# Inverse roots moved from GpSimd to ScalarE and VectorE in the first stage of a stack of graph layers

## The chip, the cores and the metric

The kernel runs on one core of a Trainium2 chip. The core has five engines with queues of their own: TensorE (PE) multiplies matrices, VectorE (DVE), ScalarE (ACT) and GpSimd (POOL) work on elements, and SyncE (SP) issues transfers. Each queue is worked off strictly in the order in which the program was written, and an instruction that needs another engine's result waits at the head of its queue. The metric is the device time of one execution in microseconds (us), the median of several runs.

## The reference

The input is `x`, 128 batches of 128 tokens with 128 features, and an adjacency matrix `adj` of 128 x 128 integers for each batch. Four graph layers follow each other. Each normalises `x` over its features (mean and variance), takes the positive part, puts it through the layer and adds the result to `x`. Cut to what matters here:

```python
def _layernorm(x, eps=1e-5):
    return (x - mean(x)) / sqrt(var(x) + eps)

h = maximum(_layernorm(x), 0)                 # layer 0
agg = sum over r of (mask_r / degree_r) @ h @ rel_weights[r]
out = agg + h @ self_w.T + self_b
x = x + relu((out - mean) * rsqrt(var + 1e-5) * ln_gamma + ln_beta)

h = maximum(_layernorm(x), 0)                 # layer 1
D = abs(h[:, :, None, :] - h[:, None, :, :])  # all pairs of tokens
s = leaky(batch_norm(D @ W1.T)) @ W2.T        # norm over all pairs of all batches
A = softmax(where(adj > 0, s, NEG))
y = leaky(batch_norm((A @ h) @ Wg.T))
x = x + concat(h, y) @ Wt.T
```

Layers 2 and 3 are attention layers with the mask `adj > 0`. So the first stage needs three norms for each token: of `x`, of the first layer's output, and of the `x` that results. It also needs the mask as bytes for the later layers.

## The kernel before, in words

The batches are worked in 32 groups of four (`G = 4`). Tokens lie on the 128 partitions; a tile of a group is 128 x 512.

The first stage does layer 0 for all groups and, at the same time, the pairwise products of layer 1. These two threads are the functions `chain` and `pairs`.

`pairs(i)` handles one of 512 tiles, four to a batch (`NT = 4`), sixteen to a group. `difference` (line 312) forms a 128 x 2048 tile `d` of differences, on VectorE for tiles 0 and 2 of a batch and on GpSimd for tiles 1 and 3 (`ON_POOL`). `absolute` (L360) takes absolute values on ScalarE, except for tile 0, which uses a maximum and extra products instead. `products` (L322, L325) multiplies on PE into PSUM. `evacuate` (L336) copies the result `hp` to `z` on ScalarE. `statistics` (L350 to L357) reads `z` on VectorE. Full halves of `z` are written to memory.

`chain(g)` handles layer 0 for a group. Its steps, with their engines, are: load `x` and `adj` (SP); `mask` (Pool, L449); moments of `x` (VectorE); inverse root and shift (Pool, `roots`); `hn` (ScalarE, `centred`, L462), which is the normalised positive part; transposition, projection and gathering (PE), with evacuations on ScalarE (L475); `joined` (VectorE, L489); moments of the output; inverse root and shift again; `oc` (ScalarE, L462); scale, offset, positive part and sum (VectorE, L493 to L497); moments of the new `x`; inverse root and shift a third time; and `h1` (ScalarE, L503), the input of layer 1. `m8` (Pool, L527) stores the mask as bytes. `features` turns `h1` into `xe` and `xw` (L394, L402), which the difference tiles and products use.

The inverse root is the helper `rsqrt` (L225, L226), which adds the epsilon and raises to the power -0.5 on GpSimd. `shift` (L281, L282) multiplies the mean by it and negates. Each works on 128 x 4 values, one for each token of a batch.

The order is written out by hand-made planning. Every piece of work is registered by `step(name, engine, cost, after, rank, work)` with a planned cost in us. `_ordered` plays the engines forward: it takes the step that can start first, with 0.4 us for each change of engine (`HOP1`), and settles ties on an engine by the rank. The resulting list is the program's order, so a changed cost or a changed step can move the work around it. Groups 0 and 1 have their chains in an opening part, which also looks for relation numbers above 1 and ends in a branch. The other 30 chains run between the pair tiles. The lines that a norm's steps come from are these:

```python
step(("rs", g), "Pool", 1.95, own("mv"), s0 + 5, roots)
step(("hn", g), "ACT", 1.55, own("rs"), s0 + 7, lambda: centred("hn", "x", AF.Relu))
```

After the first stage come a stage for layer 1's scores and sums, and one for layers 2 and 3. They use `rsqrt` too, and are not part of the change.

Of the kernel before, what the change touches and what calls it, by code (L numbers as in the profile page):

```python
# [9 lines left out]
F32 = mybir.dt.float32  # L10
# [3 lines left out]
AF = mybir.ActivationFunctionType  # L14
OP = mybir.AluOpType
AX = mybir.AxisListType

P = 128
G = 4
EPS = 1e-5  # L20
# [148 lines left out]
def tile_gnn_stack(ctx: ExitStack, tc: tile.TileContext, a: dict, out: bass.AP):  # L169
    nc = tc.nc  # L170
# [3 lines left out]
    const = ctx.enter_context(tc.tile_pool(name="const", bufs=1))  # L174
    res = ctx.enter_context(tc.tile_pool(name="res", bufs=1))
    small = ctx.enter_context(tc.tile_pool(name="small", bufs=4))
# [11 lines left out]

    ident = const.tile([P, P], F32, name="ident")
    make_identity(nc, ident)  # L190
    mhalf = const.tile([P, 1], F32, name="mhalf")
    nc.gpsimd.memset(mhalf, -0.5)
    ones = const.tile([P, P], F32, name="ones")
    nc.vector.memset(ones, 1.0)

# [21 lines left out]
    M8 = [res.tile([P, G, P], U8, tag=f"m{g}", name=f"m{g}") for g in range(NG)]  # L217
    MV1 = res.tile([P, NG, G, 2], F32, name="MV1")
    RS1 = res.tile([P, NG, G], F32, name="RS1")
# [3 lines left out]
    def rsqrt(dst, var):  # L223

        nc.gpsimd.tensor_scalar(dst, var, EPS, None, op0=OP.add)  # L225
        nc.gpsimd.tensor_tensor(dst, dst, mhalf[:, 0:1].to_broadcast(list(dst.shape)), OP.pow)  # L226
# [35 lines left out]
    with tc.tile_pool(name="c0", bufs=1) as c0, tc.tile_pool(name="p0", bufs=2) as p0, ExitStack() as ctx0:  # L262
# [11 lines left out]

        XP = [psum.tile([P, 4, P], F32, tag=f"xp{n}", name=f"xp{n}") for n in range(2)]
        gamma, beta = (t[:, 2, :] for t in XP)

        def shift(mv, rs):

            nb = small.tile([P, G], F32, name="lnnb")  # L280
            nc.gpsimd.tensor_tensor(nb, mv[:, :, 0], rs, OP.mult)  # L281
            nc.gpsimd.tensor_scalar(nb, nb, -1.0, None, op0=OP.mult)  # L282
            return nb

# [9 lines left out]
        def step(name, engine, cost, after, rank, work, takes=(), gives=()):  # L296
            steps.append((name, engine, cost, after, takes, gives, rank, work))
# [113 lines left out]
        def chain(g, agg=None, again=None):  # L411

            bs = slice(g * G, g * G + G)
            s0 = G * NT * g - 31
            t = {}
            own = lambda *names: [(name, g) for name in names]

            def tile0(name, dtype=F32, **kw):
                pool, tag = p0, name
                if again is not None:  # L420

                    pool, tag = again, {"mask": "mask4", "maskT": "adjT", "o": "adjf"}.get(name, name)
                    kw = dict(bufs=2) if name == "hn" else {}
                t[name] = pool.tile([P, G, P], dtype, tag=tag, name=name, **kw)
                return t[name]
# [8 lines left out]
            def moments(name):  # L434
                st = small.tile([P, G, 6], F32, name="lnst")
                mv = t["mv"] = MV1[:, g] if name == "MV1" else small.tile([P, G, 2], F32, name="lnmv")
                src = t["x" if name == "MV1" else name]
                for k in range(G):
                    nc.vector.bn_stats(st[:, k, :], src[:, k, :])
                for k in range(G):  # L440
                    nc.vector.bn_aggr(mv[:, k, :], st[:, k, :])

            def roots(last=False):
                rs = t["rs"] = RS1[:, g] if last else small.tile([P, G], F32, name="lnrs")
                rsqrt(rs, t["mv"][:, :, 1])
                t["nb"] = shift(t["mv"], rs)

            def masked():
                nc.gpsimd.tensor_scalar(tile0("mask"), t["adj"], 1, None, op0=OP.is_equal)  # L449
# [8 lines left out]
            def centred(dst, src, func=AF.Identity):  # L458
                if dst not in t:
                    tile0(dst)  # L460
                for k in range(G):
                    nc.scalar.activation(t[dst][:, k, :], t[src][:, k, :], func, bias=t["nb"][:, k:k + 1],  # L462
                                         scale=t["rs"][:, k:k + 1])

            def shared():
                nc.gpsimd.tensor_tensor(t["mask"], t["mask"], t["deg"][:, :, None].to_broadcast([P, G, P]),
                                        OP.mult)

            def turned(src):
                t["pt"] = sm("pt")  # L470
                for k in range(G):
                    nc.tensor.transpose(t["pt"][:, k, :], t[src][:, k, :], ident)

            def copied(name, src, func=AF.Copy):
                nc.scalar.activation(tile0(name), t[src], func)  # L475
# [34 lines left out]
            else:  # L510
# [1 line left out]
            step(("mask", g), "Pool", 1.5, own("load"), s0 + 1, masked)  # L512
            step(("mv", g), "DVE", 1.05, own("load"), s0 + 3, lambda: moments("x"))
            step(("deg", g), "DVE", 0.6, own("mask"), s0 + 3.1, degree)
            step(("rs", g), "Pool", 1.95, own("mv"), s0 + 5, roots)
            step(("most", g), "Pool", 0.25, own("deg"), s0 + 5.1, at_least)
            step(("per", g), "DVE", 0.15, own("most"), s0 + 7, lambda: nc.vector.reciprocal(t["deg"], t["deg"]))
            step(("hn", g), "ACT", 1.55, own("rs"), s0 + 7, lambda: centred("hn", "x", AF.Relu))
            step(("share", g), "Pool", 1.05, own("per"), s0 + 9, shared)
            step(("pt", g), "PE", 0.55, own("hn"), s0 + 9, lambda: turned("hn"), takes=("sm",))  # L520
            step(("hT", g), "ACT", 0.5, own("pt"), s0 + 9.5, lambda: copied("hT", "pt"), gives=("sm",))
            step(("pm", g), "PE", 0.55, own("share", "hT"), s0 + 11, lambda: turned("mask"), takes=("sm",))
            step(("maskT", g), "ACT", 0.5, own("pm"), s0 + 12, lambda: copied("maskT", "pt"), gives=("sm",))
            step(("ph", g), "PE", 1.05, own("hT") + ["small"], s0 + 11.1, projected, takes=("sm",))
            step(("hw", g), "ACT", 0.5, own("ph"), s0 + 13, lambda: copied("hw", "ph"), gives=("sm",))
            step(("m8", g), "Pool", 1.5, own("load"), s0 + 11,
                 lambda: nc.gpsimd.tensor_scalar(M8[g], t["adj"], 0, None, op0=OP.is_gt))  # L527
            step(("po", g), "PE", 2.05, own("maskT", "hw"), s0 + 14, gathered, takes=("sm",))
            step(("o", g), "DVE", 0.6, own("po", "agg") + ["selfb"], s0 + 15, joined, gives=("sm",))
            step(("mvo", g), "DVE", 1.05, own("o"), s0 + 15.1, lambda: moments("o"))  # L530
            step(("rso", g), "Pool", 1.95, own("mvo", "hn"), s0 + 17, roots)
            step(("oc", g), "ACT", 1.55, own("rso"), s0 + 18, lambda: centred("o", "o"))
            step(("on", g), "DVE", 1.25, own("oc") + ["on_all"], s0 + 20, scaled, takes=("sm",))
            step(("end", g), "DVE", 0.62, own("on"), s0 + 21, ended, gives=("sm",))
            step(("x", g), "SP", 0.4, own("end") + [("part", PARTS - 1)], s0 + 21.1, lambda: nc.sync.dma_start(X[g], t["x"]))
            step(("mvx", g), "DVE", 1.05, own("end"), s0 + 21.1, lambda: moments("MV1"))
            step(("rsx", g), "Pool", 1.95, own("mvx", "oc", "m8"), s0 + 23, lambda: roots(True))
            for half in range(2):
                step(("h1", g, half), "ACT", 0.78, own("rsx") + [("xp", 2 * g - 5)] + [("h1", g, 0)] * half,
                     s0 + 25 + half, lambda half=half: h1(half))  # L540


# [103 lines left out]
        with tc.If(nc.values_load(flag, min_val=0, max_val=1) > 0) as cmp, \  # L646
# [6 lines left out]
            for g in range(NG):  # L653
                x = pr.tile([P, G, P], F32, name="x")
                nc.sync.dma_start(x, a["x"][g * G:g * G + G].rearrange("b t c -> t b c"))
                adj = pr.tile([P, G, P], I32, name="adj")
# [3 lines left out]
                hT = pr.tile([P, G, P], F32, name="hT")  # L660
# [3 lines left out]
                o = pr.tile([P, G, P], F32, name="o")  # L664
# [107 lines left out]
    with tc.tile_pool(name="bn", bufs=1) as bn:  # L772
# [3 lines left out]
        last = bn.tile([P, 1], F32, name="last")  # L776
# [41 lines left out]
    with tc.tile_pool(name="c1", bufs=1, reuse_waits="tile") as c1, \  # L818
# [8 lines left out]
        own = c1.tile([P, 1], F32, name="own")  # L827
# [19 lines left out]
        for n in range(2):  # L847
            t = c1.tile([P, G, 1 + 2 * KH], F32, name=f"sk{n}")
# [776 lines left out]
```

## Time and profile before

| what | us |
|---|---|
| median of 3 runs | 2777.38 |
| lowest and highest run | 2776.46, 2777.83 |
| profiled execution, its own time | 2781.11 |
| its span, first to last instruction | 2779.3 |
| first stage's tiles, about | 42 to 1528 |
| of these 1486 us: VectorE busy | 1405.6 |
| ScalarE busy | 1379.5 |
| GpSimd busy | 1365.4 |
| PE busy | 1357.8 |

A profile lists every instruction with its engine, start and duration. An engine's busy time in a stretch is the time in which at least one of its instructions was running. Neighbouring instructions of an engine overlap a little, so the distance between two starts is often less than the duration. What ended an idle time is called its releaser. The chain is found by going back from the last instruction to what released it, step by step; "issue" in it is time for which the profile shows no wait. Lines such as L312 are lines of the kernel's file.

### The profile page before, as it was taken

To read this page: it belongs to the slowest core of one execution; us is meant where nothing else is said; L and a number is where in the kernel's file an instruction comes from. 1 tells how busy PE (TensorE), PEld (TensorE's weight loads), DVE (VectorE), ACT (ScalarE), POOL (GpSimd) and SP (SyncE) were. 2 spreads that over 40 slices of the span, in tenths; PEclk is the share of its full clock that TensorE was granted. 3 is DMA by queue.
4 is the path that set the end of the run, shared out by engine and by line. 5 is a ranking of instruction groups with operands and counts; after the bars stand their busy time and mean duration, and the time that the engine had idled before them with its cause. 6 is when DMAs were issued, how large, how long until landed. Compare 5 with 4: busy or idle time off the path is not lost.

```text
span 2779.3 us, 42065 instructions
## 1 busy us (share of the span) xinstructions
PE 2457.4 (88%) x14521; PEld 1182.0 (43%) x14521; DVE 2472.0 (89%) x4712; ACT 2388.7 (86%) x2837; POOL 1724.0 (62%) x1629
## 2 busy tenths in 40 slices
PE   3899999999999999999998789888888897999896
PEld 2333333333333333333332344444444445777675
DVE  4899999999999999999999688888888887899976
ACT  4899999999999999999998778778778766899985
POOL 5799999999999999999997001111000115565642
PEclk7999999999999999999999899999999999999998
DMA  7455555555555555555543899999999971121110
GB/s 283 171 223 201 212 201 210 210 212 201 208 201 208 211 209 207 208 207 215 206 193 125 330 409 411 410 411 410 409 410 410 409 266 54 46 69 58 58 31 25
DMA packets 195933, 635.66 MB, mean 229 GB/s; under 512 B 32755, under 2 KB 100470, under 8 KB 132214
## 3 DMA queue, kind: packets, MB, share of 16 engines
q1 hardware_dynamic: 195264, 632.62, 58.6%
q8 instruction: 120, 1.97, 0.3%
q14 instruction: 111, 0.91, 0.1%
q10 hardware_dynamic: 438, 0.17, 0.0%
HBM read 328.84 MB, written 303.89 MB: 228 GB/s over the span
## 4 chain that ended last, share of the span: by engine, by line
ACT 33%; PE 22%; DVE 19%; issue 11%; DMA 10%; POOL 3%; SPq 1%; ACTq 0%; DVEq 0%; POOLq 0%
ACT d L360 11%; ACT z L336 11%; PE hp L322 6%; PE ps L871 5%; DMA rows<-sk 4%; DVE d L312 3%; DMA u<-rows 3%; DVE z L914 3%; DMA z<-hp 3%; PE hp L325 2%; ACT h L1229 2%; PE pk L878 2%; PE pv L1345 2%; ACT o L462 1%; ACT h L503 1%
## 5 line engine op out<-in xcount | busy, mean ns | idle before, releaser
L312 POOL TENSOR_TENSOR d<-xe 128x2048 f32<-128x2048 f32 x256 | 1074.1, 4202 | 67.1 <-PE hp L322 48.9
L322 PE MATMUL hp<-d,w1T 128*64 128x512 f32 x4096 | 999.4, 603 | 119.8 <-ACT z L336 96.8
L360 ACT ACTIVATE d<-d 128x2048 f32<-128x2048 f32 x384 | 734.6, 1935 | 24.7 <-POOL d L312 18.2
L312 DVE TENSOR_TENSOR d<-xe,xp 128x2048 f32<-128x2048 f32 x256 | 579.5, 2264 | 5.8 <-PE hp L322 3.1
L322 PEld LDWEIGHTS hp<-d,w1T 128*64 128x64 f32 x4096 | 286.2, 137 | 640.4 <-issue 466.6
L336 ACT COPY z<-hp 128x1024 f32<-128x1024 f32 x512 | 516.9, 1028 | 47.1 <-PE hp L325 24.4
L962 POOL TENSOR_TENSOR x<-x,bt 128x512 f32<-128x512 f32 x32 | 46.5, 1455 | 672.1 <-DMA x<-x 629.0
L350 DVE BATCH_NORM_STATS2 st<-z 128x6 f32<-128x512 f32 x512 | 349.3, 682 | 42.4 <-ACT z L336 42.1
L351 DVE BATCH_NORM_STATS2 st<-z 128x6 f32<-128x512 f32 (+1 forms) x512 | 329.3, 643 | 0.0
L914 DVE SCALAR_TENSOR_TENSOR z<-z 128x2048 f32<-128x2048 f32 x128 | 296.6, 2317 | 6.5 <-ACT z L896 6.5
L896 ACT ACTIVATE z<-z,bias,scale 128x2048 f32<-128x2048 f32 x128 | 267.1, 2087 | 9.3 <-DVE bias L809 7.7
L325 PE MATMUL hp<-both_t,xw 128*64 128x512 f32 x1024 | 268.3, 596 | 0.0
L900 ACT ACTIVATE zr<-z,bias,scale 128x2048 f32<-128x2048 f32 x128 | 267.3, 2088 | 0.9 <-DMA z<-hp 0.9
L871 PE MATMUL ps<-z,w2z 128*32 128x512 f32 x1024 | 144.7, 638 | 65.1 <-DVE z L914 64.9
L878 PEld LDWEIGHTS pk<-pick,su 128*128 128x128 f32 x1024 | 127.4, 196 | 136.2 <-DVE su L892 94.0
L878 PE MATMUL pk<-pick,su 128*128 128x16 f32 x1024 | 139.9, 269 | 19.9 <-DVE su L892 19.3
L1345 PE MATMUL pv<-wr,e 128*128 128x128 f32 x1024 | 141.7, 285 | 5.8 <-DVE e L1322 4.0
L871 PE MATMUL ps<-z,w2l 128*32 128x512 f32 x1024 | 142.7, 626 | 0.0
L871 PE MATMUL ps<-zr,w2r 128*32 128x512 f32 x1024 | 141.0, 623 | 0.0
L325 PEld LDWEIGHTS hp<-both_t,xw 128*64 128x64 f32 x1024 | 80.7, 138 | 140.7 <-issue 140.7
L1345 PEld LDWEIGHTS pv<-wr,e 128*128 128x128 f32 x1024 | 129.4, 197 | 13.5 <-DVE e L1322 4.1
L1322 DVE SCALAR_TENSOR_TENSOR e<-e,ps 128x512 f32<-128x512 f32 x160 | 106.8, 677 | 25.9 <-ACT ps L1319 25.1
(243 smaller groups left out, 3823.2 us busy)
## 6 DMA issues: line engine op xcount, KB each, us to landing
hp<-z SPq DMA_DIRECT2D x248, 1024.0 KB, 3.9
z<-hp SPq DMA_DIRECT2D x248, 1024.0 KB, 14.2
x<-x SPq DMA_DIRECT2D x118, 256.0 KB, 5.9
u<-rows SPq DMA_DIRECT2D x32, 384.0 KB, 11.6
x<-in_x_dram SPq DMA_DIRECT2D x32, 256.0 KB, 3.1
adj<-in_adj_dram SPq DMA_DIRECT2D x32, 256.0 KB, 3.5
part<-in_adj_dram SPq DMA_DIRECT2D x16, 512.0 KB, 7.6
out_dram<-x SPq DMA_DIRECT2D x32, 256.0 KB, 2.4
```

What stands on the lines that cost most here:

```text
L312: eng.tensor_tensor(d, ahead, x[:, None, None, :].to_broadcast([P, 2, KC, P]), OP.max if t == BY_MAX else OP.subtract)
L322: nc.tensor.matmul(hp[64 * hh:64 * hh + 64, c:c + 512], w1T2 if by_max else w1T, d[:, hh, c:c + 512], start=True, stop=not by_max, skip_gr ...
L325: nc.tensor.matmul(hp[64 * hh:64 * hh + 64, c:c + 512], XW[i // NT // 2][:, i // NT % 2, :], both_t.rearrange("p h k i -> p h (k i)")[:, h ...
L336: nc.scalar.copy(half_of(b, t), linear.pop(i))
L350: nc.vector.bn_stats(st[:, 2 * t, :], hs[:, 0:512])
L351: nc.vector.bn_stats(st[:, 2 * t + 1, :], hs[:, 512:1024 - P * last])
L360: nc.scalar.activation(diffs[i], diffs[i], AF.Abs)
L871: nc.tensor.matmul(ps[32 * c:32 * c + 32, :], w[:, w0:w0 + 32], v[:, 512 * c:512 * c + 512], start=j0 == 0, stop=w is w2r, skip_group_chec ...
L878: nc.tensor.matmul(pk[:, kk, 0:16], su[:, kk, :], pick.rearrange("p h j -> p (h j)"), start=True, stop=True)
L900: nc.scalar.activation(zr, z1, AF.Relu, bias=bias1, scale=scale1[:, 0:1])
L914: nc.vector.scalar_tensor_tensor(z0, z0, 0.01, z0, op0=OP.mult, op1=OP.max)
L1345: nc.tensor.matmul(t[pv][:, k % 2, hd, :], t[e][:, hd, :], flat[:, at:at + P], start=True, stop=True)
```

## The change

Four things change in the first stage.

The three inverse roots of a chain are formed in another way. ScalarE takes the square root of the variance plus epsilon (`deviation`), with epsilon in a new constant column `eps`; VectorE takes the reciprocal in place (`roots`). The shift stays on GpSimd (`shifted`). Each is a step of its own.

The first norm's affine part moves from ScalarE to GpSimd (`normed`, four instructions of 128 x 128). The positive part is taken when the transposed tile is evacuated (`hT`).

The byte mask is the minimum with 1 and then the maximum with 0, in place of a comparison.

The planned costs and ranks follow, so the planner's order is made anew.

```diff
-    mhalf = const.tile([P, 1], F32, name="mhalf")
+    halves_eps = const.tile([P, 2], F32, name="mhalf")
+    mhalf, eps = halves_eps[:, 0:1], halves_eps[:, 1:2]
     nc.gpsimd.memset(mhalf, -0.5)
+    nc.gpsimd.memset(eps, EPS)
...
-            def roots(last=False):
-                rs = t["rs"] = RS1[:, g] if last else small.tile([P, G], F32, name="lnrs")
-                rsqrt(rs, t["mv"][:, :, 1])
-                t["nb"] = shift(t["mv"], rs)
+            def deviation(last=False):
+                t["rs"] = RS1[:, g] if last else small.tile([P, G], F32, name="lnrs")
+                nc.scalar.activation(t["rs"], t["mv"][:, :, 1], AF.Sqrt, bias=eps)
+
+            def roots():
+                nc.vector.reciprocal(t["rs"], t["rs"])
+
+            def shifted():
+                t["nb"] = small.tile([P, G], F32, name="lnnb")
+                nc.gpsimd.tensor_tensor(t["nb"], t["mv"][:, :, 0], t["rs"], OP.mult)
+                nc.gpsimd.tensor_scalar(t["nb"], t["nb"], -1.0, None, op0=OP.mult)
...
+            def normed():
+                tile0("hn")
+                for k in range(G):
+                    nc.gpsimd.tensor_scalar(t["hn"][:, k, :], t["x"][:, k, :], t["rs"][:, k:k + 1], t["nb"][:, k:k + 1],
+                                            op0=OP.mult, op1=OP.add)
...
-            step(("rs", g), "Pool", 1.95, own("mv"), s0 + 5, roots)
+            step(("sd", g), "ACT", 0.25, own("mv"), s0 + 4, deviation)
+            step(("rs", g), "DVE", 0.3, own("sd"), s0 + 5, roots)
+            step(("nb", g), "Pool", 0.45, own("rs"), s0 + 5.5, shifted)
...
-            step(("hn", g), "ACT", 1.55, own("rs"), s0 + 7, lambda: centred("hn", "x", AF.Relu))
+            step(("hn", g), "Pool", 1.85, own("nb"), s0 + 7, normed)
...
-            step(("hT", g), "ACT", 0.5, own("pt"), s0 + 9.5, lambda: copied("hT", "pt"), gives=("sm",))
+            step(("hT", g), "ACT", 0.5, own("pt"), s0 + 9.5, lambda: copied("hT", "pt", AF.Relu), gives=("sm",))
...
-            step(("m8", g), "Pool", 1.5, own("load"), s0 + 11,
-                 lambda: nc.gpsimd.tensor_scalar(M8[g], t["adj"], 0, None, op0=OP.is_gt))
+            step(("m8", g), "Pool", 0.8, own("load"), s0 + 11,
+                 lambda: nc.gpsimd.tensor_scalar(M8[g], t["adj"], 1, 0, op0=OP.min, op1=OP.max))
...
-            step(("rso", g), "Pool", 1.95, own("mvo", "hn"), s0 + 17, roots)
-            step(("oc", g), "ACT", 1.55, own("rso"), s0 + 18, lambda: centred("o", "o"))
+            step(("sdo", g), "ACT", 0.25, own("mvo"), s0 + 16, deviation)
+            step(("rso", g), "DVE", 0.3, own("sdo", "hn"), s0 + 17, roots)
+            step(("nbo", g), "Pool", 0.45, own("rso"), s0 + 17.5, shifted)
+            step(("oc", g), "ACT", 1.55, own("nbo"), s0 + 18, lambda: centred("o", "o"))
...
-            step(("rsx", g), "Pool", 1.95, own("mvx", "oc", "m8"), s0 + 23, lambda: roots(True))
+            step(("sdx", g), "ACT", 0.25, own("mvx"), s0 + 22, lambda: deviation(True))
+            step(("rsx", g), "DVE", 0.3, own("sdx", "oc", "m8"), s0 + 23, roots)
+            step(("nbx", g), "Pool", 0.45, own("rsx"), s0 + 23.5, shifted)
...
-                step(("h1", g, half), "ACT", 0.78, own("rsx") + [("xp", 2 * g - 5)] + [("h1", g, 0)] * half,
+                step(("h1", g, half), "ACT", 0.78, own("nbx") + [("xp", 2 * g - 5)] + [("h1", g, 0)] * half,
```

## The prediction

> **What bounds the kernel now.** I read the page's busy shares first, then busy time by stretch, then the waits and the chain inside the stretch that the change touches. The page only says that three engines are near 88% over the whole span:
>
> ```profile
> span 2779.3 us, 42065 instructions
> ...
> PE 2457.4 (88%) x14521; PEld 1182.0 (43%) x14521; DVE 2472.0 (89%) x4712; ACT 2388.7 (86%) x2837; POOL 1724.0 (62%) x1629
> ```
>
> The change lies in the first stage. There the same order of work comes back for each group of four batches: the four `hn` activations start at 715.08 us and, 15 groups later, at 1399.51, so a group takes 684.43 / 15 = 45.63 us. Busy time by stretch, of one such group, of the last group that still has a share of the chain, and of an early one (columns: length, then PE, PEld, DVE, ACT and POOL busy with counts, PE clock, DMA share, GB/s):
>
> ```profile
> 1344.87:1390.49 45.62, 42.50 (x206) 16.49 (x204) 44.24 (x77) 43.40 (x48) 43.26 (x27) 1.00 0.54 207
> 1436.11:1479.75 43.64, 39.60 (x188) 14.81 (x186) 42.70 (x67) 40.91 (x42) 36.88 (x19) 1.00 0.49 200
> 140.00:185.50 45.50, 41.62 (x192) 13.94 (x190) 45.47 (x82) 44.31 (x47) 43.75 (x27) 1.00 0.58 228
> ```
>
> All four engines are full; VectorE most, 44.24 of 45.62, so it idles 1.39 us in a group. The second line is a natural experiment: Pool is 6.4 us lighter, ACT 2.5, VectorE 1.5, and the group shortens by 2.0, with VectorE still 0.94 idle. The third shows VectorE full to 0.03. So the group's time is VectorE's work plus 0.03 to 1.39 us, depending on how the others fit. Who waits, over those 15 groups:
>
> ```profile
> PE hp L322 <- ACT z L336: 38.4, 76, 0.9
> DVE st L350 <- ACT z L336: 19.3, 30, 1.0
> POOL d L312 <- PE hp L322: 15.9, 45, 0.7
> ACT xw L402 <- DVE d L312: 13.4, 15, 1.0
> ```
>
> VectorE's named idle time is all for ScalarE's evacuation of the products, 19.3 / 15 = 1.29 us a group. ScalarE is late there because its own queue is full, as the chain inside one group shows (start, length, piece):
>
> ```profile
> 702.49 0.64 DVE st L350
> ...
> 703.84 2.19 DVE d L312
> 706.03 0.02 issue
> 706.05 0.03 ACT xw L402
> ...
> 713.42 1.81 ACT d L360
> 715.23 1.52 ACT hn L462 x4
> ...
> 720.36 1.53 ACT o L462 x4
> ```
>
> The chain runs along ScalarE through nearly the whole group, with one detour over VectorE here and one over PE at 731 us. `hn`, which the change takes from ScalarE, lies on it.
>
> **What the Trainium skill says.** "Perfetto Trace Analysis", section "Optimization Strategy", advises finding the gaps of the most-contended engine and what releases them; by that VectorE is the engine and ScalarE the releaser, which the lines above bear out. "ScalarE: Activation LUTs", section "Table sets: the hidden batching unit", says that relu, copy, identity and abs are in every table set, with sqrt the anchor of one set. The trace agrees so far as it goes: one table load of 1.28 us at 10.53 serves Relu, Copy, Identity, Abs and later Exp; a Sqrt isn't in it. The same page, section "What ACT_TABLE_LOAD costs", prices a load at 1283 ns (the trace has 1283), plus about 1380 ns of drain, which the trace doesn't show. "GPSIMD Engine Reference", section "Engine selection", calls one-input work there roughly line-rate; the trace has a 128x128 copy at 292 ns, but a 128x512 compare at 1.50 us.
>
> **The change part by part**, for one group. Three rows of the groups by shape carry most of it (output from input, count, busy us, mean ns):
>
> ```profile
> L226 POOL TENSOR_TENSOR lnrs<-lnrs,mhalf 128x4 f32<-128x4 f32 x43 | 44.6, 1037 | 3.6
> L462 ACT ACTIVATE hn<-x,lnnb,lnrs 128x128 f32<-128x128 f32 x87 | 36.3, 518 | 0.0
> L517 DVE RECIPROCAL deg<-deg 128x4 f32<-128x4 f32 x22 | 3.5, 159 | 0.0
> ```
>
> *GpSimd.* Three times the addition (227 ns) and the power (1037) go; by starts in the timeline 709.42 to 710.85, 1.43 us each, so 4.29 us. The shift's two instructions (199 and 239 ns) stay. New are four affine instructions on 128x128 with two per-partition operands. No such row exists: below, the 292 ns copy; above, the author's planned 1.85 us for four; a two-operation 128x512 on bytes takes 617 ns at its least, so (617 - 227) / 508 = 0.77 ns an element and 227 + 124 x 0.77 = 0.32 us for 128. I take 4 x 0.35 = 1.4 us, range 1.2 to 1.85. The byte mask's compare, 1.50 us, becomes a two-operation instruction: between 0.62 and 1.5, I take 0.8. Sum: -4.29 + 1.4 - 0.7 = -3.6, so 43.3 becomes 39.7 (40.8 at the dear ends). What they delay is the next difference tile behind them in that queue; with 3.6 us spare in a group that is covered, without the spare it would be paid one for one.
>
> *ScalarE.* The four `hn` go: by starts 715.08 to 716.62, 1.54 us. Three square roots on 128x4 come. The nearest row is a 128x8 copy at 186 ns; the page on ScalarE prices a pointer bias at 280 ns + 0.833 a column, an estimate of 283, less 93 of overlap. I take 0.19 each, range 0.1 to 0.28: +0.57. Relu in place of Copy on the transposed `hn` reads the same 128x512 from PSUM (661 ns), at most 0.1 more. Sum -1.0: 43.4 becomes 42.4. Were VectorE no limit, the chain along ScalarE would give 45.63 - 1.0 = 44.6.
>
> *VectorE.* Three reciprocals come. The one that is there takes 159 ns, but the next instruction starts 0.07 us after it (734.41 and 734.48 in the timeline). So 0.07 to 0.16 each; I take 0.10, +0.30: 44.24 becomes 44.54, which is more than ScalarE's 42.4 and PE's 42.5. VectorE is the bound.
>
> *The added waits.* Each reciprocal waits for a square root that stands in ScalarE's queue behind an absolute value (1.81 us between starts) or an evacuation (0.90). Behind the reciprocal on VectorE stand difference tiles and statistics, for which ScalarE and PE wait. Below nothing: the order puts it where the root is long done, as with L517, which never waited in 15 groups. Above: half an absolute value, 0.9 us each.
>
> *Order.* The written order comes from planned costs, and these change with it; planned VectorE work becomes 45.7 us a group (44.8 before, plus 0.9 for reciprocals that I price at 0.3), planned Pool and ScalarE work falls to about 41 and 42. So the order should keep VectorE's queue full, with its work placed a little later than it can run. I take an idle time of 0.70, between the 0.03 and 0.94 of the stretches above, in place of 1.39.
>
> *Sum.* 44.24 + 0.30 + 0.70 = 45.24 us a group, -0.39, times the 30 groups whose chain runs in this stretch (2 to 31): -11.7 us. The opening: its end hangs on two serial roots and shifts of 1.95 us on Pool (35.49 to 37.44 and 38.99 to 40.94); root 0.28, reciprocal 0.17, shift 0.5 and passes of 0.05 make 1.1, so 2 x 0.85 = -1.7. Two more table loads, one before the first root and one back for Exp: 2 x 1.28 = +2.6, counted whole (hidden at 0; 5.3 with the page's drain). DMA issues and their queues are untouched. Later stages keep their power function. Together -10.8, on the profiled execution's own 2781.1: 2770.3. That execution lies 3.7 above the median of the runs, 2777.4, so I forecast 2766.6.
>
> **The rivals.** *No difference:* the detour over VectorE to `xw` stays, so the idle time stays at the 0.94 of the last chain group, and the reciprocals cost their full 0.16. Then 44.24 + 0.48 + 0.94 = 45.66, 30 x 0.03 + 0.9 = +1.8: 2779. For it: that group, where relief of 6.4 us on Pool bought little. Against it: its own work differs, and an early group had none of this idle.
>
> *Slower, waits at the reciprocals:* the place is VectorE's queue at the three new instructions, the price the time that the root is late. My sum turns to a loss at 0.39 / 3 = 0.13 us of mean lateness, and at 0.18 it is beyond 0.2%. At 0.3 the group takes 44.54 + 0.70 + 0.90 = 46.14, 30 x 0.51 + 0.9 = +16: 2794; at the bound of 0.9, +70, 2847. For it: VectorE has no slack, a wait there is lost one for one, and a loaded engine's queue is now in its loop thrice. Against it: the planner allows 0.25 for the root and 0.4 for each pass, and a planned 0.3 for the reciprocal.
>
> *Table switches on each root:* if Sqrt's set lacked Abs, six loads of 1.28 a group would put 42.4 + 7.7 = 50.1 on ScalarE, 30 x 4.5 = +135: 2912. Against it is what the skill says of the sets.
>
> **How the numbers follow.** Forecast 0.48, no difference 0.20, waits 0.29, table switches 0.03. About 0.2%, 5.6 us, is what a measurement of this kernel can tell from no change; the three chances are 0.48, 0.20 and 0.32. The forecast's own range ends at 44.24 + 0.21 + 0.03 = 44.48 a group, 2744, and at 2771.8. The range over all cases is 2748 to 2804: the last tenth of the fast side is cut, and above it holds waits up to 0.41 us each.
>
> **What would show it.** Right: the group at about 45.2 us, VectorE busy near 44.5 of it, Pool near 40, ScalarE near 42.4; no wait named at the reciprocals; three table loads in all. Wrong: reciprocals in the list of waits, for ScalarE's roots, with VectorE's idle time above 1.4 a group; or VectorE idle for evacuations as before, which would mean that the new order, not the load, sets the pace; or affine instructions well over 0.5 us; or a first stage whose end moves by other than 30 times the group's difference.

## The result and the profile after

The changed kernel takes 2821.82 us, the median of four runs (2819.37 to 2823.26), where the kernel before took 2777.23 beside it. The ratio is 1.0164, with a 95% interval of 1.0152 to 1.0176. It is 45 us slower, and 18 us above the end of the predicted range. The sum was made against profiled executions: 2823.26 us with a span of 2821.5 after, 2781.11 with 2779.3 before.

The top of the page of the changed kernel, as shown of the kernel before:

```profile
span 2821.5 us, 42124 instructions
...
PE 2444.6 (87%) x14521; PEld 1182.4 (42%) x14521; DVE 2477.1 (88%) x4808; ACT 2376.1 (84%) x2806; POOL 1620.2 (57%) x1566
```

No engine but VectorE is busy longer than before, and VectorE by only 5 us, while the span is 42 us longer. So the loss is idle time, not work. The first stage holds it: its last statistics stand at 1576.2 us, in place of 1527.8, which is 48.4 us later. The later stages take 1245.3 in place of 1251.5; that they differ by some us from profile to profile is seen in the experiments too (1245 to 1252), and I don't explain it.

Inside the stage the start of `h1`, the input of layer 1, marks each group. Its lag behind the kernel before is 1.1 us in group 3, swings between 8 and 14 in groups 5 to 8, and grows by 1.83 a group from there: 8.9 in group 8, 49.4 in group 30. Busy time by stretch for one such group (columns as in the prediction: length, then PE, PEld, DVE, ACT and POOL busy with counts, PE clock, DMA share, GB/s):

```profile
719.75:767.20 47.45, 42.39 (x207) 16.62 (x206) 44.44 (x81) 43.11 (x47) 40.23 (x24) 1.00 0.50 199
```

VectorE works 44.44 us of 47.45 and idles 3.01, where it worked 44.24 of 45.62 before. The list of waits between 300 and 1300 us, 21 groups, says where (engine, line, releaser; us in total, times, longest):

```profile
...
POOL d L307 <- PE hp L317: 87.9, 106, 1.4
PE hp L317 <- ACT z L331: 75.4, 84, 1.4
DVE d L307 <- issue: 59.7, 21, 2.9
POOL xe L402 <- ACT xe L389: 42.3, 21, 2.1
ACT z L331 <- PE hp L320: 37.2, 42, 1.5
...
ACT xw L397 <- DVE d L307: 26.8, 21, 1.3
```

The line of VectorE, `DVE d L307 <- issue`, is the one to read. VectorE stands still once in each group, 59.7 / 21 = 2.84 us, at a difference tile. "Issue" says only that the profile names no releaser. No reciprocal is in the list. The second new thing is the line below it: GpSimd waits 2.0 us a group for ScalarE's `xe`, the input of the difference tiles. Both point to a late `xe`. The timeline gives that tile in its last line, and above it the pieces of the group's third root and of the way from there to the tile (start, length, engine, line, operation; idle time ahead of it in brackets):

```profile
704.35 0.37 DVE L436 BATCH_NORM_AGGREGATE MV<-lnst 128x2 f32<-128x6 f32 x4
...
705.38 0.30 ACT L440 ACTIVATE RS<-MV,mhalf 128x4 f32<-128x4 f32 x1
...
709.25 0.17 DVE L443 RECIPROCAL RS<-RS 128x4 f32<-128x4 f32 x1
...
714.23 0.21 POOL L447 TENSOR_TENSOR lnnb<-MV,RS 128x4 f32<-128x4 f32 x1
714.31 1.91 ACT L355 ACTIVATE d<-d 128x2048 f32<-128x2048 f32 x1
...
716.12 1.63 ACT L511 ACTIVATE h<-x,lnnb,RS 128x128 f32<-128x128 f32 x4
...
720.85 0.35 ACT L389 COPY xe<-xp 128x256 f32<-128x256 f32 x1
...
721.26 0.29 POOL L402 COPY xe<-xe 128x128 f32<-128x128 f32 x1 [1.98 <-ACT xe L389]
...
722.16 0.66 PE L393 MATMUL xp<-w1T,xe 128*128 128x64 f32 x4
...
722.91 2.29 DVE L307 TENSOR_TENSOR d<-xe,xp 128x2048 f32<-128x2048 f32 x1 [2.88 <-issue]
```

The moments of the new `x` are done at 704.72 us. The square root starts 0.66 us later, but the reciprocal stands behind a difference tile and statistics on VectorE and starts 3.57 us after the root's end, and the shift stands behind a mask and a difference tile on GpSimd and starts 4.81 us after the reciprocal's end. Work of 0.30 + 0.17 + 0.51 us has taken 10.0 us, from 704.72 to 714.74. Before, the power and the shift were one step:

```profile
732.96 0.36 DVE L441 BATCH_NORM_AGGREGATE MV<-lnst 128x2 f32<-128x6 f32 x4
...
737.91 1.04 POOL L226 TENSOR_TENSOR RS<-RS,mhalf 128x4 f32<-128x4 f32 x1
...
739.32 0.24 POOL L282 TENSOR_SCALAR lnnb<-lnnb 128x4 f32<-128x4 f32 x1
...
742.06 0.88 ACT L503 ACTIVATE h<-x,lnnb,RS 128x128 f32<-128x128 f32 x2
```

From moments at 733.32 to the shift's end at 739.56 this took 6.2 us. In the changed kernel `h1` follows at 716.12, 11.4 us after the moments (before: 8.7), and VectorE has run out of statistics at 720.0 and has nothing else ahead of the tile that needs `h1`.

The profile shows no wait of `h1` for the shift. In all 17 groups between 500 and 1300 us ScalarE goes over to it without idle time from an absolute value (714.31 here), which itself starts as GpSimd's tile ends. The lateness lies in the places that the plan gave to the pieces in the queues, and so no instruction of the root need be seen waiting.

Behind `h1` the way goes on over PE, ScalarE and GpSimd. In each of the 17 gaps between 500 and 1300 us the tile starts 0.09 us after the end of PE's product of `xe` (L393, which writes the PSUM tile `xp` that the difference tile reads), and 1.2 to 1.4 us after GpSimd's copy of `xe`. So the wait without a name most likely ends with this product. Of the two the plan lets the tile wait for the copy alone. Nearly half of the gap lies behind that copy, and no run takes this part away.

The chain passes over the same pieces:

```profile
704.95 3.96 POOL d L307
708.91 0.17 issue
709.07 1.04 POOL mask L474
710.11 4.17 POOL d L307
714.28 0.02 issue
714.31 0.02 ACT d L355
714.33 1.79 issue
716.12 1.33 ACT h L511 x4
```

It no longer runs along ScalarE through nearly the whole group, but here along GpSimd, whose tile holds up both the shift and the absolute value ahead of `h1`. GpSimd is idle 7.2 of 47.45 us, the most of the four engines: the least loaded one, entered at a bad moment.

### The profile page after: what moved, and what is told of

It is laid out like the page before. It is cut to its first block, busy times and chain, and to the rows that moved or that the text cites. A ratio compares the mean times of both kernels' runs of the same rounds, so it can differ in the third digit from the quotient of the medians.

```text
span 2821.5 us, 42124 instructions
## 1 busy us (share of the span) xinstructions
PE 2444.6 (87%) x14521; PEld 1182.4 (42%) x14521; DVE 2477.1 (88%) x4808; ACT 2376.1 (84%) x2806; POOL 1620.2 (57%) x1566
## 4 chain that ended last, share of the span: by engine, by line
PE 27%; DVE 23%; ACT 15%; POOL 14%; DMA 12%; issue 7%; SPq 0%; POOLq 0%; DVEq 0%; ACTq 0%
POOL d L307 10%; PE hp L317 10%; DVE d L307 5%; DMA rows<-sk 4%; PE ps L885 4%; ACT d L355 4%; DMA u<-rows 4%; DVE z L928 3%; DMA z<-hp 3%; PE hp L320 3%; ACT z L331 2%; DVE st L345 2%; DVE st L346 2%; ACT h L1243 2%; PE pk L892 2%
## 5 line engine op out<-in xcount | busy, mean ns | idle before, releaser
L307 POOL TENSOR_TENSOR d<-xe 128x2048 f32<-128x2048 f32 x256 | 1075.2, 4200 | 151.0 <-PE hp L317 150.8
L307 DVE TENSOR_TENSOR d<-xe,xp 128x2048 f32<-128x2048 f32 x256 | 580.0, 2266 | 83.6 <-issue 80.1
L331 ACT COPY z<-hp 128x1024 f32<-128x1024 f32 x512 | 509.5, 1010 | 76.8 <-PE hp L320 49.9
## 6 DMA issues: line engine op xcount, KB each, us to landing
z<-hp SPq DMA_DIRECT2D x248, 1024.0 KB, 14.2
```

Of the source, the lines that this page charges most:

```text
L307: eng.tensor_tensor(d, ahead, x[:, None, None, :].to_broadcast([P, 2, KC, P]), OP.max if t == BY_MAX else OP.subtract)
L331: nc.scalar.copy(half_of(b, t), linear.pop(i))
```

## Experiments

One theory is that the new order of the program sets the pace, by making the third root late (**order**). Its rival is that the new instructions do, by waits and contention that the loads don't show (**instructions**). No kernel leaves out a part of the computation.

**The work of before in the new order.** Steps, costs and ranks are those of the changed kernel; at the place of each piece stands the work of the kernel before, and the places of roots and reciprocals are empty. PE's instructions stand one by one as in the changed kernel.

```diff
-            step(("sdx", g), "ACT", 0.25, own("mvx"), s0 + 22, lambda: deviation(True))
-            step(("rsx", g), "DVE", 0.3, own("sdx", "oc", "m8"), s0 + 23, roots)
-            step(("nbx", g), "Pool", 0.45, own("rsx"), s0 + 23.5, shifted)
+            step(("sdx", g), "ACT", 0.25, own("mvx"), s0 + 22, nothing)
+            step(("rsx", g), "DVE", 0.3, own("sdx", "oc", "m8"), s0 + 23, nothing)
+            step(("nbx", g), "Pool", 0.45, own("rsx"), s0 + 23.5, lambda: powered(True))
```

> The steps, costs and ranks of the changed kernel, so its order, but at each place the work of the kernel before: the power on GpSimd where the shift stands, the affine part with Relu on ScalarE where GpSimd's stands, the comparison for the byte mask; nothing at the places of the square root and the reciprocal. Theory A: slow as the changed kernel, 2800 to 2840, with the idle time at the first difference tile. Theory B: back near the kernel before, 2770 to 2790.

Measured: 2830.79 us, ratio 1.0189 (1.0172 to 1.0206). Its list of waits, 500 to 1300 us, some 17 groups:

```profile
DVE d L307 <- issue: 46.8, 17, 2.8
```

The same gap, 2.75 us a group, without a square root, reciprocal or affine instruction of the change in the stage. The order alone costs 53 us; the instructions then give 9 back. This carries the verdict.

**The change's work in the old order.** The reverse: steps, costs and ranks of before, with the change's instructions at each place.

```diff
-                rsqrt(rs, t["mv"][:, :, 1])
+                nc.scalar.activation(rs, t["mv"][:, :, 1], AF.Sqrt, bias=eps)
+                nc.vector.reciprocal(rs, rs)
...
-            step(("hn", g), "ACT", 1.55, own("rs"), s0 + 7, lambda: centred("hn", "x", AF.Relu))
+            step(("hn", g), "ACT", 1.55, own("rs"), s0 + 7, normed)
```

> The mirror of the last swap: steps, costs and ranks of the kernel before, so its order (PE's is the same instruction by instruction), with the change's work at each place: square root, reciprocal and shift where the power and shift stood, the affine part on GpSimd where ScalarE's stood, the new byte mask. Theory A (the order costs the time, the instructions don't): a group takes 44.7 to 45.7 us and the total is 2750 to 2782. Theory B (the instructions cost it by their waits): 2800 or more, with VectorE idle ahead of the reciprocals, which here stand right behind their square roots in the program and have no room planned for the round trip.

Measured: 2781.16 us, ratio 1.0016 (1.0009 to 1.0023). Its `h1` starts at 1021.56, 1066.76, 1111.96 and 1157.16 us: 45.20 a group, the forecast's 45.24. VectorE is busy 786.4 us of the 800 from 500 to 1300, which is 44.43 a group and leaves 0.77 idle. Of the gain of 0.43 a group nothing is left at the end, since the groups ahead of 434 us lose it: `h1` stands at 433.90 there, 11.2 later than before. The waits of 140 to 440 us on VectorE:

```profile
DVE lnrs L448 <- ACT lnrs L447: 8.5, 6, 2.3
```

With 5.8 us more for the third root, 14.3 us of waits at the reciprocals stand in six early groups. In the even part, 500 to 1300 us, there are 8.4 in 17 groups, 0.5 each.

Two parts of the change were also put into the old order singly: the three roots alone, and the affine part on GpSimd alone.

> As the last one, but only the three inverse roots are new; the affine part stays on ScalarE and the byte mask is a comparison. Theory A: 2765 to 2785. Theory B: the loss comes from here, 2795 or more.

> The order of the kernel before; only the first norm's affine part is moved to GpSimd and the positive part to the evacuation. ScalarE is 1.5 us a group lighter, GpSimd 1.7 heavier, and has 2.4 to spare. Theory A: 2760 to 2780. Theory B makes no claim on it; if the affine part is what hurts, 2790 or more, with GpSimd's difference tiles late.

Measured: 2795.96 us (1.0069, 1.0051 to 1.0087) for the roots, 2802.41 (1.0089, 1.0072 to 1.0106) for the affine part. Each alone costs 20 to 26 us, both and the byte mask together 5. Both times lie in the ranges that stood for the new instructions as the cause: in an order that was made for other loads a part of the change costs time, although the whole nearly doesn't. With the affine part alone, GpSimd is busy 773 of 800 us, and ScalarE's absolute values wait 39.0 us, 2.3 a group, for its difference tiles; the roots alone take three times 1.43 us a group off GpSimd, and put three times 0.30 on ScalarE, where `hn` still stands. Each part makes the room that the other one fills. That is read from loads and waits; no run took the room away by itself.

**Which root.** The changed kernel with the second or the third root as before (one step of 1.95 us on GpSimd; the order is made anew).

```diff
-            step(("sdx", g), "ACT", 0.25, own("mvx"), s0 + 22, lambda: deviation(True))
-            step(("rsx", g), "DVE", 0.3, own("sdx", "oc", "m8"), s0 + 23, roots)
-            step(("nbx", g), "Pool", 0.45, own("rsx"), s0 + 23.5, shifted)
+            step(("nbx", g), "Pool", 1.95, own("mvx", "oc", "m8"), s0 + 23, lambda: powered(True))
```

> Only the third inverse root, the one ahead of the next layer's input, is again one step on GpSimd; the rest is as changed. Theory A: a good part of the loss goes, since this root is the last thing ahead of the late tile; 2770 to 2795. Theory B: each of the three roots costs a third, so about 15 us come back, 2800 to 2812.

> Only the second inverse root, that of the first layer's output, is again one step on GpSimd. Theory A: the planner leaves the same gap ahead of the first difference tile, so little comes back, 2805 to 2825. Theory B: a third of the loss comes back, 2800 to 2812; both are near each other here, and the sign is whether VectorE still idles 2 to 3 us a group at that tile (A) or not (B).

Measured: with the third root undone 2798.10 us (1.0066, 1.0049 to 1.0083), and the gap without a releaser falls to 0.2 us in 17 groups (14.8 us of waits with names stand at that tile in its place); with the second undone 2829.87 (1.0185, 1.0168 to 1.0202), and the gap stays, 49.1 us in 17 groups. So the gap hangs on the third root, and 24 of the 45 us go with it. The kernel with the second root undone is 8 us slower than the changed one and above both of its ranges, which its new order may explain; no run tests it.

**Which queue.** Of the changed kernel's third root only the shift is moved: from GpSimd to VectorE, behind the reciprocal and in the same step.

```diff
+            def roots_and_shift():
+                roots()
+                t["nb"] = small.tile([P, G], F32, name="lnnb")
+                for k in range(G):
+                    nc.vector.tensor_scalar(t["nb"][:, k:k + 1], t["mv"][:, k, 0:1], t["rs"][:, k:k + 1], -1.0,
+                                            op0=OP.mult, op1=OP.mult)
...
-            step(("rsx", g), "DVE", 0.3, own("sdx", "oc", "m8"), s0 + 23, roots)
-            step(("nbx", g), "Pool", 0.45, own("rsx"), s0 + 23.5, shifted)
+            step(("rsx", g), "DVE", 0.5, own("sdx", "oc", "m8"), s0 + 23, roots_and_shift)
```

> The changed kernel with only the third root's shift moved: VectorE forms it behind the reciprocal, in four instructions on 128x1 that read one tensor and one pointer, in one step planned at 0.5 us; GpSimd has no step between the third root and h1. Theory (the third full queue on the third root's way makes the next layer's input late): from the third moments to the input one wait of a queue fewer, about 6 to 8 us in place of 10.0, so VectorE's idle time ahead of the group's first difference tile falls from 2.8 us to under 1.5, the group to 46.0-46.6 and the time to 2780-2805. Rival (the lateness comes from the change's other edits or from more load): the idle time stays near 2.8, the group near 47.4, and the time is 2810-2830. If these instructions too are held up by GpSimd's tiles, as the one instruction with two tensors was, they take over 1 us each and the time is above 2850.

Measured: 2783.13 us, ratio 1.0021 (1.0014 to 1.0028), 39 us faster than the changed kernel, although VectorE gets four instructions more. Its waits on VectorE, 500 to 1300 us, and two lines of its timeline:

```profile
DVE d L307 <- issue: 4.7, 8, 0.6
```

```profile
502.53 0.36 DVE L436 BATCH_NORM_AGGREGATE MV<-lnst 128x2 f32<-128x6 f32 x4
...
507.63 0.58 DVE L449 TENSOR_SCALAR lnnb<-MV,RS 128x1 f32<-128x1 f32 x4
```

From moments to shift 502.89 to 508.21, 5.3 us, less than the 6 to 8 expected. With one queue fewer on the way the gap is down to 0.28 us a group.

**The planned costs.** The changed kernel with the planned costs set near what the trace shows: reciprocal 0.08 in place of 0.3, square root 0.2 for 0.25, `hn` 1.75 for 1.85, byte mask 0.65 for 0.8.

```diff
-            step(("rsx", g), "DVE", 0.3, own("sdx", "oc", "m8"), s0 + 23, roots)
+            step(("rsx", g), "DVE", 0.08, own("sdx", "oc", "m8"), s0 + 23, roots)
```

> The changed kernel with planned costs nearer to the measured ones: 0.2 for the square root, 0.08 for the reciprocal, 1.75 for the affine part, 0.65 for the byte mask (0.25, 0.3, 1.85 and 0.8 in the change). Only the order differs. Theory A: the time moves with the order; the planner's own clock then has 46.3 us a group in place of 47.8, so 2775 to 2805. Theory B: within 6 us of the changed kernel, 2816 to 2828.

Measured: 2789.33 us (1.0047, 1.003 to 1.0064). Not one instruction differs from the changed kernel's, and 32 us of its 45 are gone. The path by way of three queues is the same; in this order it meets them at better moments (8.7 us from moments to `h1`).

**The ranks of the chains.** The rank of a chain's steps against the pair tiles hangs on one number. In the changed kernel:

```diff
-            s0 = G * NT * g - 31
+            s0 = G * NT * g - 37
```

> All of the change's instructions and planned costs stay; only the ranks of the whole chain are six tiles earlier, so the planner makes another order. Theory A (the order: the third norm's output comes too late for the first difference tile of the next group, and VectorE stands 2.9 us idle there in each group): the idle time goes, a group takes 44.6 to 45.3 us in place of 47.45, the total is 2735 to 2765. Theory B (the instructions: square roots, reciprocals and shifts in three full queues cost their waits wherever they are put): the total stays above 2800.

Measured: 2808.82 us (1.0118, 1.0101 to 1.0135). The gap at the difference tile is gone, and most of the loss is still there. PE now pauses about once a group for ScalarE's evacuation, and the stretches after one of these pauses show another loss:

```profile
715.00:718.00 3.00, 0.60 (x6) 0.05 (x2) 2.72 (x4) 3.00 (x4) 2.91 (x3) 1.00 0.00 0
718.00:720.00 2.00, 2.00 (x6) 0.83 (x8) 2.00 (x3) 2.00 (x2) 1.75 (x4) 0.51 0.74 299
720.00:722.00 2.00, 2.00 (x8) 0.67 (x6) 2.00 (x5) 0.91 (x2) 0.23 (x1) 0.63 0.57 221
```

After a pause of 2.40 us the granted clock of PE is 0.51 and 0.63, and twelve products take 4.49 us; the eight just ahead of the pause took 1.94. The Trainium skill, "TensorE: Matmul & The Clock Gate", section "Part 1: The HAM clock gate", says that the clock is halved after an idle window of about 3.4 us; the trace agrees on the halving, with a pause shorter than that. Not every pause has this sequel. Between 500 and 1300 us PE pauses 26 times for 1.8 to 3.2 us; 12 of the pauses are followed by half the clock for 3.4 us, and others of 2.40 and 2.98 us are not. From the end of a pause of 1.82 us to the end of the next, of 2.40, it takes 25.05 us with the low clock (509.72 to 534.77) and 23.35 without (602.18 to 625.53). At 1.7 us each, the 12 cost an estimated 20 of the 800 us. The kernels before and changed have no such pause there. With the corrected costs of the run before it and this rank, the loss turns:

> All of the change's instructions, planned costs near the measured ones, the chain six tiles earlier. Planner's own clock: 45.3 us a group. Theory A: 2755 to 2785, so the change's instructions need not be slower than the kernel before. Theory B: 2800 or more.

Measured: 2761.41 us (0.9949, 0.993 to 0.9967): all of the change's instructions, and faster than before. And the kernel before, with its own instructions, and its chains 8 places earlier:

```diff
-            s0 = G * NT * g - 31
+            s0 = G * NT * g - 39
```

> The kernel before, its own instructions and costs, with the ranks of its chain eight tiles earlier; another order alone. The planner's own clock has 44.83 us a group in place of 45.51. If the planner's clock can be trusted to 0.3 us (as for five of the six orders run so far): 2745 to 2765. If, as with the chain six tiles earlier in the changed kernel, PE's pauses and its clock take it back: 2770 to 2790.

Measured: 2737.41 us, ratio 0.9859 (0.9839 to 0.9879), faster than both expectations. This is the best kernel of the study, 84 us ahead of the changed one. The stretch 500 to 1300 us, and the longest waits of PE's products and of ScalarE in it:

```profile
500.00:1300.00 800.00, 763.30 (x3690) 288.67 (x3688) 797.91 (x1378) 784.39 (x853) 779.60 (x471) 1.00 0.55 214
```

```profile
PE hp L322 <- ACT z L336: 35.4, 63, 1.2
...
ACT z L336 <- PE hp L322: 15.3, 34, 0.8
```

VectorE is busy 797.91 of 800 us and a group takes 44.24, as long as VectorE was busy in a group of the kernel before. Here the load is the bound.

**The change's work in that best order.** As in the old order above, each new instruction at the place of the piece that it replaces.

> All the change's instructions, each at the place of the piece that it replaces, in the order that the kernel before gets when its chains are ranked 8 places earlier (2737.4 us with its own instructions, VectorE busy 797.9 of 800 us). If VectorE alone bounds that order, three reciprocals of 0.1 to 0.17 us add 0.3 to 0.5 us a group, and 2746-2755 results, with no wait of over 0.5 us a group at the reciprocals. If the roots are late there too, as in the opening third of the old order, over 10 us of named waits stand at the reciprocals and the time is 2755-2790. If the lighter GpSimd and ScalarE queues pay in this order, 2720-2735.

Measured: 2803.55 us (1.0086, 1.0068 to 1.0104), 66 us slower than the same order with the old instructions, and outside all three expectations. The waits, 500 to 1300 us:

```profile
POOL lnnb L283 <- DVE lnrs L448: 57.5, 25, 3.2
...
POOL lnnb L283 <- DVE RS L448: 28.8, 9, 3.2
```

Waits at the reciprocals were expected, and 12.3 us stand there at the third root. The longer ones stand one step on, where GpSimd holds its queue for the reciprocal, 86.3 us or 5 a group; two thirds of them belong to the first two roots. In the old order with the new work the same two lines have 66.9 us, 3.9 a group, at 45.20 us a group. What is worse here are the waits of ScalarE's absolute values for GpSimd's difference tiles, 26.2 us in place of 10.9 there. That GpSimd's waits make its tiles late, and these the loss, is read from the lists; no run shows it.

The lateness of the third root explains little of the 66 us. With the power on GpSimd `h1` starts 3.4 us after the moments, in the mean; with the round over three engines it is 3.9, and in every other group that round takes only 1.8 us from the moments to the shift's end.

**The shift on VectorE in one instruction.** All three shifts, each as one `scalar_tensor_tensor` of 128x4 behind its reciprocal; GpSimd's shift steps are gone. Then the same with the earlier rank of 37 and a planned cost of 0.2.

```diff
-                nc.gpsimd.tensor_tensor(t["nb"], t["mv"][:, :, 0], t["rs"], OP.mult)
-                nc.gpsimd.tensor_scalar(t["nb"], t["nb"], -1.0, None, op0=OP.mult)
+                nc.vector.scalar_tensor_tensor(t["nb"], t["mv"][:, :, 0], -1.0, t["rs"], op0=OP.mult, op1=OP.mult)
```

> The changed kernel with the shift made on VectorE, in one instruction right behind the reciprocal, in place of two on GpSimd; so a root passes two queues and no longer three. It adds some 0.1 us a root on VectorE. Theory A, in the form that the third root's way through a third full queue makes the next layer's input late: the idle time at the group's first difference tile goes, the group takes 46.1 us as the planner's own clock has it, and the total is 2770 to 2798. If the lateness is not from the shift's queue: 2810 to 2830.

> The shift on VectorE as above, planned at 0.2 us with its reciprocal, and the chain six tiles earlier. Planner's own clock: 45.4 us a group with VectorE never idle. Theory A: 2755 to 2785; Theory B: 2800 or more.

Measured: 2935.88 us (1.0586, 1.0556 to 1.0616) and 2911.48 (1.0488, 1.0468 to 1.0508), the slowest of all. The timeline of the first:

```profile
718.57 4.21 POOL L307 TENSOR_TENSOR d<-xe 128x2048 f32<-128x2048 f32 x1 [1.40 <-PE hp L317]
...
721.27 1.53 DVE L445 SCALAR_TENSOR_TENSOR lnnb<-lnmv,lnrs 128x4 f32<-128x4 f32 x1
...
746.28 4.19 POOL L307 TENSOR_TENSOR d<-xe 128x2048 f32<-128x2048 f32 x1
...
747.27 3.22 DVE L445 SCALAR_TENSOR_TENSOR lnnb<-MV,RS 128x4 f32<-128x4 f32 x1
```

Here four elements a partition take 1.53 and 3.22 us, and each ends 0.02 us after GpSimd's running tile (722.80 and 722.78; 750.49 and 750.47). The whole kernel has 96 of these instructions (count | busy us, mean ns):

```profile
L445 DVE SCALAR_TENSOR_TENSOR lnnb<-MV,RS 128x4 f32<-128x4 f32 x32 | 97.7, 3052 | 1.1
L445 DVE SCALAR_TENSOR_TENSOR lnnb<-lnmv,lnrs 128x4 f32<-128x4 f32 x64 | 97.3, 1521 | 2.2
```

68 of the 96 take over 0.3 us, and each of these ends 0.02 us after a GpSimd instruction with two inputs; the shortest of the others take 0.16 us. The Trainium skill, "SBUF — State Buffer", section "SBUF: two separate sides", says that a VectorE instruction with two SBUF inputs and a GpSimd instruction that reads SBUF share a pair of ports, which one holds for its whole length. The trace agrees. In the run above four instructions with one tensor and a pointer, on the same data, took 207 ns each, and at most 216, although 28 of the 128 lie wholly inside a difference tile of GpSimd. So the edit tested the ports and not the queue, which was then tested as shown.

The kernels side by side. The second column is the mean time from the third moments to `h1`, the third the time without a releaser at VectorE's difference tiles for each group, the fourth the mean group, all between 500 and 1300 us (with the third root undone, where groups of 41, 47 and 51 us alternate, over five whole turns):

| kernel | median us | moments to `h1` | gap | group |
|---|---|---|---|---|
| before | 2777 | 8.7 | none | 45.63 |
| changed | 2821.8 | 11.5 | 2.8 | 47.46 |
| old work, new order | 2830.8 | 11.7 | 2.8 | 47.53 |
| second root undone | 2829.9 | 11.5 | 2.9 | 47.72 |
| third root undone | 2798.1 | 6.9 | 0.0 | 46.44 |
| third shift on VectorE | 2783.1 | 8.1 | 0.3 | 45.95 |
| planned costs corrected | 2789.3 | 8.7 | 0.4 | 46.07 |
| before, ranks 8 earlier | 2737.4 | 3.4 | none | 44.24 |

Among these kernels the gap is there when `h1` comes over 11 us after the moments, and nearly gone below 9. With earlier ranks 11.7 us leave no such gap, since `h1` is then planned ahead of its need; the loss moves to PE, as shown.

## Why the prediction was wrong

**The loads** were nearly right. VectorE's work was put at 44.54 us a group and is 44.44, GpSimd's at 39.7 and is 40.23, ScalarE's at 42.4 and is 43.11: of the 1.0 us by which ScalarE was to get lighter, 0.3 came. The reading that ScalarE was late because its queue was full left out a line of the same list, ScalarE's own wait for PE (`ACT z L336 <- PE hp L325`, 14.2 us in 15 groups). The new operations, by shape, 300 to 1300 us (count | busy us, mean ns):

```profile
L470 POOL TENSOR_SCALAR hn<-x,lnrs,lnnb 128x128 f32<-128x128 f32 x84 | 36.6, 448 | 2.2
L537 POOL TENSOR_SCALAR m<-adj 128x512 uint8<-128x512 int32 x22 | 13.5, 612 | 0.0
L440 ACT ACTIVATE lnrs<-lnmv,mhalf 128x4 f32<-128x4 f32 x42 | 12.5, 299 | 1.1
L443 DVE RECIPROCAL lnrs<-lnrs 128x4 f32<-128x4 f32 x42 | 6.9, 165 | 0.0
```

The affine instruction takes 448 ns for 350, the byte mask 612 for 800, the square root 299 for 190, a little over the range. The reciprocal's 165 is as expected, with the next instruction 0.08 us behind its start (709.25 and 709.33). None of these decides.

**The table loads** were put at three and are two, 1.28 us each: the first operation of ScalarE that needs a table is now the square root itself, so no load is added ahead of it. No switch of sets occurs at the roots, as the Trainium skill ("ScalarE: Activation LUTs", section "Table sets: the hidden batching unit") led the prediction to expect by putting relu, copy, identity and abs in every set.

**The opening** was to gain 1.7 us. Group 0's `h1` is 1.9 us earlier, but group 1's is 4.5 later and group 2's 2.2. I costed the two serial roots and not the round of the second one over three queues.

**Order** is the step that failed: "So the order should keep VectorE's queue full, with its work placed a little later than it can run. I take an idle time of 0.70". It is 3.01. The term was taken from stretches of the old order, and its lower end of 0.03 from one that is no group: where 140 to 185.5 us was read, the first difference tiles of the groups are 49 and 41 us apart, and the stretch holds 82 VectorE instructions, where an even group has 77. For the new order I argued from planned loads, that the engine with most planned work would have no gaps. But the planner takes what can start first and looks no further, and the third root of a group decides when the first difference tile of the next layer's group can start. Its three steps each join a queue of tiles, of 1.9 us on ScalarE, 2.3 on VectorE and 4.2 on GpSimd. From the moments to `h1` it now takes 11.4 us in place of 8.7, and VectorE stands 2.84 us idle at that tile in each group. The prediction's own sign for this was "VectorE idle for evacuations as before, which would mean that the new order, not the load, sets the pace": VectorE is idle, not for evacuations but for the root. With an idle time near 0.70 the sum holds: in the old order the new work takes 45.20 us a group, with 0.77 idle. There the total fails all the same, by the early groups.

**The rival of waits at the reciprocals** (2794) had the sign, and is not what happened: the changed kernel has no named wait there. Its mechanism is real where the order is not made for it: 14.3 us at the reciprocals in the old order's early groups. Its argument against itself, that the planner allows for the root, is what keeps those waits out of the changed kernel, and the same caution makes the path longer; that is read from the plan and the order, and only the corrected costs, 32 us faster, speak for it. It had looked for the price at the instruction that waits; it stood at the end of the path.

**What stays open.** Every edit of a step makes the whole order anew. So the runs show that the new order makes the gap, and that a third root in one step, a shorter path and corrected costs each mend it, but not that one entry of the plan is the culprit, nor what the wait for PE's product of `xe` is worth by itself. Why the same new work costs 66 us in the best order isn't shown either. Whether the new instructions can reach 2737 in an order of their own is open; the best found was 2761.

## What to carry to other kernels

When an edit splits one step into three on three engines, price the way as well as the work: look up how long the tiles are that each of the queues holds, and ask who runs dry at the end of that way. Where a program's order is made by planned costs, run the old work in the new order and the new work in the old one before you judge an instruction; here the new order cost 53 us with the old instructions and 41 with the new, and the same new instructions cost 5 us in one order of the old work and 66 in another. An engine with spare time is no shortcut when a 4.2 us tile stands at its head.

## What the runs showed of the hardware

- A VectorE instruction of 128x4 with two tensors in SBUF took 1.5 us in the mean at the first two roots and 3.05 at the third. The 68 of 96 that took over 0.3 us all ended 0.02 us after a GpSimd instruction with two inputs, in a kernel 4.0% slower than the changed one. With one tensor and a pointer such an instruction took 207 ns.
- The byte mask on GpSimd by minimum and maximum takes 612 ns, the comparison took 1.50 us, on the same 128x512.
- After 12 of 26 pauses of 1.8 to 3.2 us PE was granted half its clock for 3.4 us, at a price of 1.7 us each where it can be compared. The length of the pause alone doesn't tell which: one of 1.82 us had it, others of 2.98 us had not.
